# Operand order, a moved transpose and a moved copy at the start of a cross-attention block

## The chip, the cores and the metric

The kernel runs on one core of a Trainium2 chip. The metric is the time of one execution on the device in microseconds (us), as the median of several runs. The core has four engines that compute: TensorE (PE, matrix products and transposes), VectorE (DVE), ScalarE (ACT) and GpSimd (POOL). A fifth, SyncE (SP), issues nearly all data transfers (DMA) here. Each engine works through its own queue of instructions and waits on semaphores for the others. Matrix products are written to PSUM, the accumulators, and copied from there to SBUF, the working memory.

## The reference

All numbers are float32. `x` has 8 sequences of 256 tokens with 512 features; `ctx` has the same shape; the mask is all ones.

```python
x = layer_norm(hidden_states, ln1_w, ln1_b)
q = x @ q_w + q_b
k = encoder_hidden_states @ k_w + k_b
v = encoder_hidden_states @ v_w + v_b            # 16 heads of 32 features each
attn = softmax(where(mask, q k^T / sqrt(32), -max))
out = (attn v) @ cproj_w + cproj_b
hidden = out + residual
y = layer_norm(hidden, ln2_w, ln2_b)
y = gelu(y @ fc_w + fc_b) @ proj_w + proj_b      # 512 -> 2048 -> 512
return hidden + y
```

## The kernel before, in words

The eight sequences are worked in four groups `g` of two, so a group has 512 tokens: four tiles of 128. Weights and transposed tokens are kept as four quarters, "11", "12", "21" and "22", each of 128 partitions x 2 chunks x 256 columns. The first digit of a weight quarter is the half of the outputs and the second the half of the features that are summed over; for tokens the first digit is the half of the features and the second the half of the tokens. Most projections use a Strassen scheme (`strassen`, seven products in place of eight), which needs sums of quarters (`sum_up`, L171). DVE and POOL form these.

The keys of group 0 are the exception. They are needed before any sums can be ready, so `eight` (L455) multiplies the plain quarters. One call makes one quarter of the keys in one PSUM tile of two 256-column halves `i`; it adds over four feature chunks `c`. The profile shows each of these matrix products as two instructions, so a quarter has 16.

The order of all work is written out by hand: each engine's queue is the order in which the Python code calls it. The start of the kernel is this order (L804 and on):

- `warm`: twelve transposes of the identity matrix on PE.
- SP issues the loads: ctx tiles 0 and 1, key weights "11" and "12" (`kw`), ctx tiles 2 and 3, key weights "21" and "22", then x of group 0, the query weights `qw`, the mask, the value weights `vw`, two bias vectors (`cb`, `projb`), ctx of group 1, and the weights `cw` of the output projection. POOL issues eight small loads into `rows`, one 128-wide row for each 128 entries of the bias and scale vectors.
- `turn_first_ctx` (L309) has two pieces. Piece 0 transposes ctx tiles 0 and 1 and makes ctx quarters "11" and "21"; piece 1 transposes tiles 2 and 3 and makes "12" and "22". In each, DVE copies the first quarter (L324) and ACT the second (L326).
- The run `first[0], k[0], first[1], k[1]` puts piece 0 ahead of key quarter "11" and piece 1 between the key quarters "11" and "12".
- In the middle of quarter "12", `turn_cols` (L479) transposes `rows` on PE, and DVE copies the result to `cols`, so that every vector stands as one column per 128 entries. Then ACT adds the key bias, which is one of these columns, to quarter "11", which had waited for it (`waiting`).
- Then come `seen` (layer-norm statistics of x, four tiles, DVE, L194), `roots` (1/sqrt of the variances, POOL, L199 and L200), key quarter "21", `normalise` (DVE, L203), the sums of `qw`, the mask, `tx` (transposes of x on PE, L216, scaled on the way out of PSUM by ACT and DVE), key quarter "22", and the seven query products `q`.

The key quarters "21" and "22" go to DRAM (`store_quarter`, L420); SP issues these stores in its one queue, and `load_x(1)`, the load of x for group 1, stands in that queue behind the second of them. The statistics of x of group 1 are called between the query products, so on DVE they stand between the additions u2 and u3 of the Strassen scheme (L391, L400). After the values, the kernel goes through 32 attention units (scores, softmax, transposed probabilities, product with the values) with the projections of later groups spread between them, and then through the two feed-forward products of each group.

Of the kernel before, what the change touches and what calls it, by code (L numbers as in the profile page):

```python
# [16 lines left out]
P = 128  # L17
# [5 lines left out]
def tile_xattn_block(  # L23
# [45 lines left out]
    nc = tc.nc  # L69
# [9 lines left out]
    NC = D // P  # L79
# [6 lines left out]
    HI, HC, HF, HD2 = INNER // 2, NC // 2, NF // 2, D // 2  # L86
# [27 lines left out]
    n_rows = sum(n for _, n in vecs)  # L114
    rows = const.tile([n_rows, P], F32, name="rows")
    cols = const.tile([P, n_rows], F32, name="cols")
    at, col_of = 0, []
# [6 lines left out]
    def col(base, i):  # L124
        return cols[:, base + i : base + i + 1]
# [4 lines left out]
    QUARTERS = ("11", "12", "21", "22")  # L130
# [87 lines left out]
    def tokens_operand(pool, tag, name):  # L218
        return Operand(pool.tile([P, 7, HC, S], F32, tag=tag, bufs=1, name=name))
# [29 lines left out]
    with ExitStack() as att:  # L249
# [8 lines left out]
        ctxs, xs, att_in, ws, pts = {}, {}, {}, {}, {}  # L258
# [15 lines left out]
        def turned(name):  # L274


            places[0] += 1
            if not pts and (places[0] % 2 or probs):
                return ps_t.tile([P, G], F32, tag="pt", name=name)
            return ps_s.tile([P, G], F32, tag="s", name=name)  # L280
# [28 lines left out]
        def turn_first_ctx():  # L309


            def piece(k):
                if k == 0:
                    ctxT[0] = tokens_operand(both, "cT", "ctxT_0")
                for j in range(2):
                    ps = turned(f"pct_0_{k}_{j}").rearrange("p (c s) -> p c s", c=HC)
                    for t in range(2):
                        for c in range(HC):
                            nc.tensor.transpose(
                                ps[:, c, ts(t, P)], ctxs[0][2 * k + t][:, ts(HC * j + c, P)], ident  # L320
                            )
                    to = ctxT[0][QUARTERS[2 * j + k]]
                    if j == 0:
                        nc.vector.tensor_copy(to, ps)  # L324
                    else:
                        nc.scalar.copy(to, ps)  # L326

            return [lambda k=k: piece(k) for k in range(2)]

        def turn_x(g):  # L330
            def piece(c):
                if c == 0:
                    xnT[g] = tokens_operand(work, "xT", f"xnT_{g}")
                ps = turned(f"pxt_{g}_{c}")
                turn(ps, xs[g], c)
                if g == 0 and c % 2:
                    nc.vector.tensor_scalar(
                        chunk(xnT[g], c), halves(ps), col(c_ln1w, c), col(c_ln1b, c), ALU.mult, ALU.add
                    )
                else:  # L340
                    nc.scalar.activation(
                        chunk(xnT[g], c), halves(ps), AF.Identity,
                        bias=col(c_ln1b, c), scale=col(c_ln1w, c),
                    )

            return [lambda c=c: piece(c) for c in range(NC)]

        turns, later, waiting = [0], [], []
# [68 lines left out]
        def store_quarter(g, tag, o, k, st):  # L417
            d = qkv_dram[g, tag]
            d = d[k * S : (k + 1) * S, ts(o, S)] if tag == "v" else d[o * S : (o + 1) * S, ts(k, S)]
            nc.sync.dma_start(d.rearrange("(i p) s -> p i s", p=P), st)  # L420

        def staged(g, tag, n):
            return work.tile([P, 2, S], F32, tag="st", bufs=3, name=f"st_{tag}_{g}_{n}")

        def project_qk(g, tag):
            w, base = ("k", c_kb) if tag == "kT" else ("q", c_qb)

            def made(n, bank, u):
                o, k = int(n[0]) - 1, int(n[1]) - 1

                direct = g == 0 and o == 0
                st = None if direct else staged(g, tag, n)
                for i in range(2):
                    b = col(base, 2 * o + i)
                    to = qk[g, i, tag][:, ts(k, S)] if direct else st[:, i, :]
                    if u is None:
                        nc.scalar.activation(to, bank[:, i, :], AF.Identity, bias=b, scale=1.0)
                    else:
                        nc.vector.scalar_tensor_tensor(
                            to, bank[:, i, :], b, u[:, i, :], ALU.add, ALU.add  # L440
                        )
                if not direct:
                    store_quarter(g, tag, o, k, st)

            def src():
                return (ctxT if tag == "kT" else xnT)[g]

            if g == 0:
                for i in range(2):
                    qk[g, i, tag] = work.tile([P, G], F32, tag=tag, name=f"{tag}_{g}_{i}")  # L450
            if g == 0 and tag == "kT":
                return [lambda n=n: eight(f"p{tag}_{g}", n, ws[w], src, made) for n in QUARTERS]
            return strassen(f"p{tag}_{g}", lambda: ws[w], src, False, made)

        def eight(name, n, w, x, made):  # L455


            bank = ps_m.tile([P, 2, S], F32, tag=f"m{turns[0]}", name=f"{name}_{n}")
            turns[0] ^= 1
            for i in range(2):  # L460
                if n == "12" and i == 1:

                    turn_cols()
                    waiting.pop()()
                for c in range(NC):
                    nc.tensor.matmul(  # L466
                        bank[:, i, :],
                        w[f"{n[0]}{c // HC + 1}"][:, c % HC, ts(i, P)],
                        x()[f"{c // HC + 1}{n[1]}"][:, c % HC, :],
                        start=i == 0 and c == 0,  # L470
                        stop=c == NC - 1,
                        skip_group_check=True,
                    )
            if n == "11":
                waiting.append(lambda: made(n, bank, None))
            else:
                made(n, bank, None)

        def turn_cols():  # L479
            ps = turned("ps_cols")  # L480
            nc.tensor.transpose(ps[:, :n_rows], rows, ident[:n_rows, :n_rows])
            nc.vector.tensor_copy(cols, ps[:, :n_rows])

        def project_v(g):

            def made(n, bank, u):
                o, k = int(n[0]) - 1, int(n[1]) - 1
                st = staged(g, "v", n)
                if u is None:
                    nc.scalar.copy(st, bank)  # L490
                else:
                    nc.vector.tensor_tensor(st, bank, u, ALU.add)
                store_quarter(g, "v", o, k, st)

            return strassen(f"pv_{g}", lambda: ws["v"], lambda: ctxT[g], True, made)
# [185 lines left out]
        def load_ctx(g):  # L681
            ctxs[g] = load_tiles(work, group_of(ef, g), "ctx", f"ctx_{g}")
# [72 lines left out]
        g = 1  # L755
        begin(g, 0, 3, load_res, 0, *QUARTERS)
        begin(g, 2, 2, bias_res, 0)
        g = 2
# [6 lines left out]
        g = NG - 1  # L765
# [33 lines left out]
        def run(pieces):  # L799
            for p in pieces:  # L800
                p()
# [15 lines left out]
        for to, vec in ((cb, cproj_b), (projb, proj_b)):  # L817
            nc.sync.dma_start(to, vec.partition_broadcast(P))

        first = turn_first_ctx()  # L820
        k, q, v, tx = project_qk(0, "kT"), project_qk(0, "qT"), project_v(0), turn_x(0)
        seen, roots, normalise = layer_norm(xs[0], "a0")
        run([first[0], k[0], first[1], k[1]])
        load_ctx(1)
        ws["c"] = weight("cw", cproj_w)
        run([*seen, roots, k[2], *normalise])
# [71 lines left out]
    with ExitStack() as mlp:  # L898
# [39 lines left out]
        for g in range(NG):  # L938
# [28 lines left out]
            for q in range(HF // 2):  # L967
                bank = {
                    n: ps_f.tile([P, 2, S], F32, tag=f"f{n}", name=f"pf{n}_{g}_{q}") for n in (1, 6, 7, 5)
                }  # L970
# [59 lines left out]
            if g + 1 < NG:  # L1030
# [4 lines left out]
            bank = {  # L1035
                n: ps_f.tile([P, 2, HD2], F32, tag=f"f{n}", name=f"py{n}_{g}") for n in (1, 6, 7, 5)
            }
# [104 lines left out]
```

## Time and profile before

| | us |
|---|---|
| median of 3 runs | 755.97 (755.66 to 756.12) |
| the profiled execution's own time | 755.82 |
| its span, first to last instruction | 754.0 |
| PE busy | 745.0 |
| POOL busy | 380.2 |
| DVE busy | 361.2 |
| ACT busy | 293.4 |
| first key product starts | 6.06 |
| key quarter "12" starts | 10.97 |
| transposes of x start on PE | 18.68 |
| first query product starts | 24.98 |

The profile is of one execution. Times in its views count from the first instruction, and the span is 1.8 us shorter than the execution's own time. A row of a timeline gives the start, the length, the engine, the line of the kernel, and what is written and read; a note in square brackets gives the engine's idle time just before it and who ended it. The chain of waits is followed back from the last instruction: at each step it goes to whatever released that instruction, or to the one ahead of it on the same engine. In the rows of DMA issues the last number is the time from issue to landing.

### The profile page before, as it was taken

How to read it: one execution, taken by the hardware profiler on the slowest of the kernel's cores; microseconds unless marked ns; L12 is line 12 of the kernel's file. 1: busy time of each engine (PE TensorE's matmuls, PEld its weight loads, DVE VectorE, ACT ScalarE, POOL GpSimd, SP SyncE). 2: the span in 40 equal slices, each digit the busy share in tenths (PEclk: the TensorE clock that was granted, in tenths of full speed). 3: DMA queues.
4: the chain of work that ended last, by engine and by line, in shares of the span. 5: the costliest groups of instructions: out<-in, count | busy, mean ns of one | idle time of the engine just before them, and what ended most of it. 6: DMA issues, size and time to landing. Idle time of an engine off the chain costs nothing.

```text
span 754.0 us, 12115 instructions
## 1 busy us (share of the span) xinstructions
PE 745.0 (99%) x4437; PEld 625.1 (83%) x4437; DVE 361.2 (48%) x970; ACT 293.4 (39%) x851; POOL 380.2 (50%) x346
## 2 busy tenths in 40 slices
PE   8999999999999999999999999999999999999997
PEld 7888777888788776778888888888888888888886
DVE  2776755676466566765355542245422255122111
ACT  2277777765776777761341002230013300032100
POOL 3857679677564479896654420126202165012540
PEclk9999999999999999999999999999999999999999
DMA  9714522642234268433930003000040000200001
GB/s 300 227 65 130 166 81 81 185 165 85 85 104 154 85 194 265 129 113 98 295 123 1 1 29 140 1 1 0 1 167 1 1 1 0 82 31 0 1 1 56
DMA packets 60331, 68.70 MB, mean 91 GB/s; under 512 B 5060, under 2 KB 46064, under 8 KB 60144
## 3 DMA queue, kind: packets, MB, share of 16 engines
q1 hardware_dynamic: 60016, 67.91, 27.6%
q8 instruction: 35, 0.57, 0.3%
q14 instruction: 24, 0.20, 0.1%
q0 software_dynamic: 256, 0.02, 0.0%
HBM read 46.95 MB, written 20.97 MB: 90 GB/s over the span
## 4 chain that ended last, share of the span: by engine, by line
PE 94%; ACT 2%; DVE 2%; issue 1%; DMA 1%; POOL 0%; SPq 0%; DVEq 0%; POOLq 0%
PE py L914 26%; PE pf L914 26%; PE ppt L617 7%; PE pqT L367 6%; PE pv L367 5%; PE po L367 5%; PE s L564 5%; PE av L633 5%; PE pkT L367 5%; ACT pr L592 2%; PE pkT L466 1%; PE pyt L216 1%; PE pxt L216 1%; ACT pt L622 1%; PE pct L216 1%
## 5 line engine op out<-in xcount | busy, mean ns | idle before, releaser
L914 PE MATMUL pf<-y,fcw 128*128 128x256 f32 x896 | 194.0, 379 | 0.0
L914 PEld LDWEIGHTS pf<-y,fcw 128*128 128x128 f32 x896 | 170.2, 190 | 23.1
L606 POOL TENSOR_TENSOR pr<-pr,rsum 128x512 f32<-128x512 f32 x128 | 130.3, 1050 | 75.5 <-DVE rsum L604 44.3
L592 ACT ACTIVATE pr<-pr,nmax 128x256 f32<-128x256 f32 x256 | 128.1, 503 | 61.3 <-DVE nmax L582 61.2
L1018 POOL TENSOR_TENSOR hs<-h,h 128x512 f32<-128x512 f32 x16 | 20.3, 1268 | 192.4 <-PE pf L914 146.7
L582 DVE CUSTOM_DVE_ANT_0 pr<-s,mb 128x256 f32<-128x256 f32 x256 | 94.1, 413 | 42.0 <-PE s L564 32.8
L914 PE MATMUL py<-pw,h 128*128 128x256 f32 x384 | 85.1, 380 | 0.0
L914 PE MATMUL py<-pw_t,h 128*128 128x256 f32 x384 | 83.5, 379 | 0.0
L914 PEld LDWEIGHTS py<-pw,h 128*128 128x128 f32 x384 | 72.7, 190 | 10.0
L914 PEld LDWEIGHTS py<-pw_t,h 128*128 128x128 f32 x384 | 72.7, 190 | 9.8
L993 ACT COPY u<-pf 128x512 f32<-128x512 f32 x16 | 9.4, 586 | 166.3 <-PE pf L914 164.7
L617 PEld LDWEIGHTS ppt<-ident,pr 128*128 128x128 f32 x512 | 57.3, 141 | 14.8 <-issue 9.9
L617 PE MATMUL ppt<-ident,pr 128*128 128x128 f32 x512 | 68.7, 276 | 0.2
L622 ACT COPY pt<-ppt 128x512 f32<-128x512 f32 x96 | 51.7, 572 | 4.9 <-PE ppt L617 4.9
L977 ACT ACTIVATE h<-h,cols 128x256 f32<-128x256 f32 x96 | 43.4, 501 | 25.8 <-DVE h L1014 13.3
L367 PE MATMUL pv<-vw,ctxT 128*128 128x256 f32 x224 | 52.4, 380 | 0.0
L977 ACT ACTIVATE h<-pf,cols 128x256 f32<-128x256 f32 x32 | 13.4, 471 | 99.6 <-PE pf L914 99.6
L367 PE MATMUL pqT<-xnT,qw 128*128 128x256 f32 x224 | 51.0, 379 | 0.0
L592 ACT ACTIVATION_READ_ACCUMULATOR pr<-pr,nmax 128x1 f32 x256 | 48.5, 189 | 0.0
L367 PEld LDWEIGHTS pqT<-xnT,qw 128*128 128x128 f32 x224 | 41.4, 190 | 5.0
L367 PEld LDWEIGHTS pv<-vw,ctxT 128*128 128x128 f32 x224 | 41.0, 190 | 5.4 <-issue 0.3
L633 PE MATMUL av<-pt,v 128*32 128x256 f32 x512 | 38.9, 386 | 1.3 <-ACT pt L622 0.4
(132 smaller groups left out, 966.9 us busy)
## 6 DMA issues: line engine op xcount, KB each, us to landing
ctx<-in_ctx_dram SPq DMA_DIRECT2D x16, 256.0 KB, 4.6
x<-in_x_dram SPq DMA_DIRECT2D x16, 256.0 KB, 4.1
v_dram<-st_v SPq DMA_DIRECT2D x16, 256.0 KB, 2.2
v<-v_dram SPq DMA_DIRECT2D x16, 256.0 KB, 3.7
resx<-in_x_dram SPq DMA_DIRECT2D x16, 256.0 KB, 5.2
hid_dram<-resx SPq DMA_DIRECT2D x16, 256.0 KB, 2.3
hm<-hid_dram SPq DMA_DIRECT2D x16, 256.0 KB, 5.9
fcw<-in_L_xattn_fc_w_dram SPq DMA_DIRECT2D x16, 256.0 KB, 6.0
```

What stands on the lines that cost most here:

```text
L216: nc.tensor.transpose(ps[:, ts(t, P)], xt[:, ts(c, P)], ident)
L367: nc.tensor.matmul(bank[n][:, i, :], l[:, c, ts(i, P)], r[:, c, :], start=first and i == 0 and c == 0, stop=last and c == HC - 1, skip_gro ...
L564: nc.tensor.matmul(banks[j][:, i, :], qT[j * HD : (j + 1) * HD, b * S + i * P : b * S + (i + 1) * P], kT[j * HD : (j + 1) * HD, b * SK : ( ...
L582: nc.vector.tensor_tensor_reduce(pr[:, j, i, :], banks[j][:, i, :], mbias[g][1][:, b, :], scale=-SCALE, scalar=FLT_MAX, op0=ALU.add, op1=A ...
L592: nc.scalar.activation(pr[:, j, i, :], pr[:, j, i, :], AF.Exp, bias=nmax[:, j, i : i + 1], scale=-1.0, accum_out=sums[:, j, i : i + 1],)
L606: nc.gpsimd.tensor_tensor(pr[:, j], pr[:, j], rsum[:, j, :, None].to_broadcast([P, NQ, SK]), ALU.mult,)
L617: nc.tensor.transpose(ps[:, kc, ts(i, P)], probs[n][:, j, i, ts(kc, P)], ident)
L622: nc.scalar.copy(pt, ps)
L633: nc.tensor.matmul(av[j * HD : (j + 1) * HD, :], vs[g, hg][:, b * NK + kc, ts(j, HD)], pts[n, j][:, kc, :], start=(kc == 0), stop=(kc == N ...
L914: nc.tensor.matmul(ps, lhsT, rhs, start=first, stop=last, skip_group_check=True)
L977: nc.scalar.activation(h[n][q][:, i, :], src[:, i, :], AF.Gelu_apprx_tanh, bias=col(c_fcb, half * HF + 2 * q + i), scale=1.0,)
L1018: nc.gpsimd.tensor_tensor(h["s3"][q], h["11"][q], h["21"][q], ALU.subtract)
```

## The change

Three things are changed, all in the first four key quarters and the call that runs them.

- `eight` goes through the products in another order: first all that read the first half of the features (both column halves `i`), then all that read the second half. The number of products is the same. A table of `hooks` may name places between products at which something else is run.
- The second piece of the ctx transposes is no longer called between the key quarters "11" and "12". It is run inside quarter "11", ahead of its seventh product (of eight).
- The vectors are turned ahead of the fifth product of quarter "12", as before, but their copy out of PSUM is made by ACT in place of DVE.

```diff
-                return [lambda n=n: eight(f"p{tag}_{g}", n, ws[w], src, made) for n in QUARTERS]
+                return [lambda n=n: eight(f"p{tag}_{g}", n, ws[w], src, made, FIRST_KEYS.get(n, {})) for n in QUARTERS]
...
-        def eight(name, n, w, x, made):
+        def eight(name, n, w, x, made, hooks):
...
-            for i in range(2):
-                if n == "12" and i == 1:
-
-                    turn_cols()
-                    waiting.pop()()
-                for c in range(NC):
-                    nc.tensor.matmul(
-                        bank[:, i, :],
-                        w[f"{n[0]}{c // HC + 1}"][:, c % HC, ts(i, P)],
-                        x()[f"{c // HC + 1}{n[1]}"][:, c % HC, :],
-                        start=i == 0 and c == 0,
-                        stop=c == NC - 1,
-                        skip_group_check=True,
-                    )
+
+            for at, (j, i, c) in enumerate((j, i, c) for j in range(2) for i in range(2) for c in range(HC)):
+                if at in hooks:
+                    hooks[at]()
+                nc.tensor.matmul(
+                    bank[:, i, :],
+                    w[f"{n[0]}{j + 1}"][:, c, ts(i, P)],
+                    x()[f"{j + 1}{n[1]}"][:, c, :],
+                    start=at == 0,
+                    stop=j == 1 and c == HC - 1,
+                    skip_group_check=True,
+                )
...
+        def turn_second_half():
+            first_ctx[1]()
+
+        def turn_vectors():
+
+            turn_cols()
+            waiting.pop()()
+
+        FIRST_KEYS = {"11": {6: turn_second_half}, "12": {4: turn_vectors}}
+
         def turn_cols():
             ps = turned("ps_cols")
             nc.tensor.transpose(ps[:, :n_rows], rows, ident[:n_rows, :n_rows])
-            nc.vector.tensor_copy(cols, ps[:, :n_rows])
+            nc.scalar.copy(cols, ps[:, :n_rows])
...
-        first = turn_first_ctx()
+        first_ctx = turn_first_ctx()
...
-        run([first[0], k[0], first[1], k[1]])
+        run([first_ctx[0], k[0], k[1]])
```

## The prediction

> **What bounds the kernel now.** I read the page first (busy shares), then the chain that ended last in order of time, because the change touches only the first 23 us and a share over the whole span hides them.
>
> ```profile
> PE 745.0 (99%) x4437; PEld 625.1 (83%) x4437; DVE 361.2 (48%) x970; ACT 293.4 (39%) x851; POOL 380.2 (50%) x346
> ```
>
> TensorE (PE) is busy 745 of 754 us, so only what moves PE's own stream counts. The chain over the first 26 us:
>
> ```profile
> 1.65 4.27 DMA kw<-in_L_xattn_k_w_dram
> 5.92 0.14 issue
> 6.06 3.69 PE pkT L466 x16
> 9.75 0.45 PE pct L319 x4
> ...
> 10.22 0.70 DVE ctxT L324
> 10.93 0.04 issue
> 10.97 1.99 PE pkT L466 x8
> ...
> 13.19 0.20 DVE cols L482
> 13.39 0.61 DVE st_a L194
> ...
> 17.00 1.05 POOL rstd_a L200
> ...
> 18.54 1.47 DVE x L203 x3
> 20.00 0.04 issue
> 20.05 1.64 PE pxt L216 x13
> 21.69 3.46 PE pkT L466 x16
> ```
>
> The chain leaves PE twice. At 10.2 it goes to VectorE (DVE), which copies the turned ctx half for quarter "12". At 13.2 it goes to DVE and GpSimd (POOL) for x's layer norm and returns at 20.05. A matmul here is two instructions; 16 in 3.46 us means one per 0.216 us. After 25 us the chain is PE almost without a break to 53.6.
>
> The size of the second hole: quarters "12" and "21" end at 13.18 + 24 x 0.216 = 18.36 (13.08, plus 0.10 of restart). The 16 turns of x at 0.109 would end at 20.10; the next quarter starts at 21.53. Lost: 1.42 us. Why is the norm late? From the timeline of DVE, then the DMA issues in the window 4.65 to 4.75:
>
> ```profile
> 10.22 0.69 DVE L324 COPY ctxT<-pct 128x512 f32<-128x512 f32 x1 [4.76 <-PE pct L319]
> 13.19 0.20 DVE L482 COPY cols<-ps_cols 128x44 f32<-128x44 f32 x1 [2.27 <-PE ps_cols L481]
> 13.31 0.68 DVE L194 BATCH_NORM_STATS2 st_a<-x 128x6 f32<-128x512 f32 x1
> ```
> ```profile
> x<-in_x_dram SPq DMA_DIRECT2D x1, 256.0 KB, 5.9
> ```
>
> x's first tile was issued at 4.60 and landed 5.9 us later, at 10.5. DVE was free at 10.9, but the copy of the turned vectors stood ahead of the statistics in its queue and waited 2.27 us for PE.
>
> [...]statistics whose data lay there waited behind a copy. [...]the keys' store at 21.20 landed only 7.2 us later behind the loads ahead of it, the one at 26.05 in 2.7.
>
> **The change part by part.**
>
> *Order of the first quarter.* The old order used kw "12" from its fifth instruction, the new from its ninth. kw "11" landed at 5.92 and started PE; kw "12", issued at 2.12, landed 4.5 us later at 6.6, and the fifth instruction started about 6.9 without a wait. So the order itself is worth 0. ScalarE's (ACT) copy of ctx "21" ended at 5.8, also hidden. In quarter "12" the order only puts off the need for ctx "22" (ACT's copy ended at 11.24) to instruction nine.
>
> *Second half of ctx turned inside the quarter.* The 8 turns (0.87 us) move from behind 16 instructions to behind 12, from 9.59 to 6.06 + 0.07 + 12 x 0.216 = 8.72. The tiles they need were issued at 2.63 and 3.10 and landed 4.9 and 5.0 later, 7.5 and 8.1: no wait, 0.6 to spare. DVE's copy started 0.64 after the first turn and PE went on 0.75 after that start: 8.72 + 0.64 + 0.75 = 10.11. Meanwhile PE ends the turns at 9.59 and the last four key instructions at 10.46. So quarter "12" starts at 10.46 without a wait, against 10.97, and its restart (second instruction 0.32 after the first, not 0.216) goes too: **0.61 us** gained. Cover gone (copy over 0.35 late): the old wait returns in part, at most 0.61. No DMA is moved.
>
> *Turned vectors, copied by ACT.* They still stand after eight instructions of quarter "12", now about 12.3. The last bias row, issued at 5.36, landed 5.8 later at 11.2: no wait. The gap of about 0.4 around this 44-row turn stays. On ACT the copy ([...]below nothing it can't be, above it 0.3 by the 0.586 of a twelve times larger copy) runs about 12.6 to 12.8, then the two bias additions for quarter "11" (0.84) to 13.7. Behind them only quarter "21" waits, which needs the bank at 14.3: 0.6 to spare, so 0. ACT has nothing else queued. DVE loses 0.20.
>
> *What that frees.* DVE ends ctx "12" at 10.05 and begins the statistics when x lands, 10.6. They need 0.80 a tile; the fourth tile landed at 12.4 and is wanted at 13.0. From the first statistics to the roots took 13.31 to 18.05 = 4.74, so normalising runs 15.4 to 17.3 (1.92). POOL was idle for 10.8 us ahead of it. PE ends quarter "21" at 18.36 - 0.61 = 17.75 and finds all four tiles: **1.42 us** gained, 0.45 to spare. Without ACT's copy, DVE's would stand at 12.6 and about 1.4 of this be lost again.
>
> *What is late next.* PE's x turns 17.75 to 19.50, last key quarter to 22.95, queries from there (24.98 before): 2.03. DVE's sums end 17.3 + 5.35 (20.00 to 25.35 before) = 22.65, wanted by the second product at 24.7. POOL's sums follow DVE's and move 2.5 to 2.7. These are free. The exception is load_x(1): SyncE (SP) issues it behind the store of the last key quarter, so it moves from 26.52 to 24.5, but its tiles then queue behind cw and the stores. On DVE its statistics stand ahead of u3, which the sixth query product needs:
>
> ```profile
> 29.38 0.69 DVE L194 BATCH_NORM_STATS2 st_a<-x 128x6 f32<-128x512 f32 x1
> 31.05 0.69 DVE L194 BATCH_NORM_STATS2 st_a<-x 128x6 f32<-128x512 f32 x1 [0.76 <-DMA x<-in_x_dram]
> 32.09 0.69 DVE L400 TENSOR_TENSOR pqT_u<-pqT,pqT_u 128x512 f32<-128x512 f32 x1
> ```
> ```profile
> x<-in_x_dram SPq DMA_DIRECT2D x1, 256.0 KB, 4.0
> ```
>
> The second tile was issued at 27.03 and landed 4.0 later, 31.03. In the new time the sixth product starts at 22.95 + 5 x 1.73 = 31.6, so u3 must start by 30.9 and the second statistics (0.93 ahead) by 29.9. Earliest: issue at 25.0 plus the store's 2.7 as shortest landing, 27.7; no loss. Latest: unmoved, 31.05; loss 1.1 plus 0.1 restart, 1.2. Taken: the first tile no earlier than about 29.3, since the last quarter of cw, issued at 20.34, landed only 7.1 later[...]; and the second statistics 0.80 after it, 30.1: **0.2 lost**.
>
> Sum: 0.61 + 1.42 - 0.2 = 1.83. The profiled execution took 755.82 (span 754.0, 1.8 around it), so 753.99. The median of the runs shown is 0.15 higher: 754.14, said as **754.1**.
>
> **Rivals.**
>
> *Whole shift.* x(1) lands in time: 2.03 gained, 753.9. For: DMA was near idle at 26 to 27, so the tiles can start a microsecond earlier.[...] With 0.5 lost instead it is 754.4; I count both as the forecast.
>
> *x(1) sets the queries.* It lands where it did: 2.03 - 1.2 = 0.83, 755.1.
>
> *The norm does not move.* DVE or POOL is held by something unshown, and only the 0.61 stays: 755.4. Against: no wait on anything but PE stands ahead of the statistics.
>
> *Slower: x(1) later than before.* The same place and price: each us past 29.9 for the second statistics stops PE for one. It decides at 29.9 + 2.03 = 31.9, 0.9 later than in the profile, where new and old are even; from 33.4 it costs over 0.2%. For: the loads enter busier DMA queues.[...]
>
> *More.* The attention stage has waits of ACT in PE's weight loads (9.6 us before the attention products); another phase there could add or take 0.3 to 0.5: 753.5.
>
> **How the numbers follow.** Forecast with its spread 753.8 to 754.4: 0.57. More than that gained: 0.10. x(1) sets the queries, or a part of the gain is lost later: 0.17. Norm doesn't move: 0.10. Slower: 0.06. About 0.2% (1.5 us) is what a measurement of this kernel can tell from no change; 754.46 is that bound. Faster is the first two and a third of the third: 0.72; same 0.22; slower 0.06. The range 753.5 to 755.3 leaves out the slower case and the far ends.
>
> **What would show it.** Right: turns of ctx at 8.7, key quarter "12" at 10.5 with no wait on DVE; statistics at 10.6 waiting on DMA, not PE; x's turns at about 17.8 with no idle time; queries at about 23.0; everything from 35 us on early by one amount. Wrong: PE idle in the queries behind u3 with x(1) named; a wait on ctx inside the first quarter; bias additions holding quarter "21"; or the early amount shrinking through the attention units.

## The result, and the profile after

The changed kernel takes 754.29 us (median of 12 runs, 753.90 to 755.44), the kernel before 756.06 us in the same comparison (12 runs). The ratio is 0.9977, with a 95% interval of 0.9968 to 0.9986: 1.8 us or 0.23% faster. The forecast was 754.1, in a range of 753.5 to 755.3. The profiled execution of the changed kernel took 754.31 us, with a span of 752.5.

The page's row of busy time, changed kernel: TensorE does the same work in a shorter span.

```profile
PE 744.8 (99%) x4437; PEld 626.2 (83%) x4437; DVE 360.5 (48%) x969; ACT 293.1 (39%) x852; POOL 380.0 (50%) x346
```

The chain of waits in order of time, changed kernel (start, length, what):

```profile
1.64 4.42 DMA kw<-in_L_xattn_k_w_dram
6.06 0.14 issue
6.19 3.18 PE pkT L464 x12
9.37 0.87 PE pct L319 x8
10.25 2.59 PE pkT L464 x12
12.84 0.19 PE ps_cols L489
13.03 5.38 PE pkT L464 x24
18.40 1.75 PE pxt L216 x16
20.15 3.46 PE pkT L464 x16
23.61 12.16 PE pqT L367 x56
```

Both of the chain's ways out of PE are gone: it stays on PE from the landing of the key weights on. The second half of ctx is turned behind 12 key instructions and key quarter "12" follows without a gap. The 16 turns of x follow quarter "21" at once.

The timeline of DVE, changed kernel, shows why the norm is no longer late:

```profile
9.85 0.69 DVE L324 COPY ctxT<-pct 128x512 f32<-128x512 f32 x1 [4.09 <-PE pct L319]
11.04 0.69 DVE L194 BATCH_NORM_STATS2 st_a<-x 128x6 f32<-128x512 f32 x1 [0.49 <-DMA x<-in_x_dram]
15.82 1.92 DVE L203 TENSOR_SCALAR x<-x,mv_a,rstd_a 128x512 f32<-128x512 f32 x4 [1.49 <-POOL rstd_a L200]
```

The statistics wait for the landing of x and for nothing else, where they waited for PE's turn of the vectors before. They start at 11.04 in place of 13.31.

What is due to the change and what to the execution? PE's timeline, first of the kernel before, then of the changed one:

```profile
3.98 1.20 PE L319 MATMUL pct<-ident,ctx 128*128 128x128 f32 x8
6.06 3.69 PE L466 MATMUL pkT<-ctxT,kw 128*128 128x256 f32 x16 [0.88 <-DMA kw<-in_L_xattn_k_w_dram]
24.98 12.25 PE L367 MATMUL pqT<-xnT,qw 128*128 128x256 f32 x56
```
```profile
3.97 1.91 PE L319 MATMUL pct<-ident,ctx 128*128 128x128 f32 x8
6.19 3.18 PE L464 MATMUL pkT<-ctxT,kw 128*128 128x256 f32 x12 [0.31 <-DMA kw<-in_L_xattn_k_w_dram]
23.44 12.33 PE L367 MATMUL pqT<-xnT,qw 128*128 128x256 f32 x56
```

The queries start 1.54 us sooner. But the same eight ctx turns took 1.91 us here and 1.20 before: PE runs at half pace at first (its warming transposes start 0.213 us apart in both profiles, later ones 0.109). The trace's record of the granted clock has full speed from 6.9 us on in this execution, against 4.3. So the first two key instructions took 0.86 us, start to start, in place of 0.51. The key weights also landed at 6.06 in place of 5.92. These two, 0.35 and 0.13, belong to the execution. Without them the queries would start at 22.96, where the prediction had 22.95. From there the lead holds: the first scores stand at 37.43 against 38.89 (1.46), and the spans differ by 1.5.

### The profile page after: what moved, and what is told of

Same layout as the page of the kernel before. It is cut to its first block, busy times and chain, and to the rows that moved or that the text cites. A ratio compares the mean times of both kernels' runs of the same rounds, so it can differ in the third digit from the quotient of the medians.

```text
span 752.5 us, 12116 instructions
## 1 busy us (share of the span) xinstructions
PE 744.8 (99%) x4437; PEld 626.2 (83%) x4437; DVE 360.5 (48%) x969; ACT 293.1 (39%) x852; POOL 380.0 (50%) x346
## 4 chain that ended last, share of the span: by engine, by line
PE 94%; ACT 2%; DMA 2%; DVE 1%; issue 0%; SPq 0%; DVEq 0%
PE py L922 26%; PE pf L922 26%; PE ppt L625 7%; PE pqT L367 6%; PE pv L367 6%; PE s L572 5%; PE po L367 5%; PE pkT L367 5%; PE av L641 5%; PE pkT L464 2%; ACT pr L600 1%; PE pyt L216 1%; PE pxt L216 1%; PE pct L216 1%; DMA kw<-in_L_xattn_k_w_dram 1%; ACT pt L630 1%
```

## The experiments

**One part alone: the ScalarE copy.** The kernel before with one line changed.

```diff
-            nc.vector.tensor_copy(cols, ps[:, :n_rows])
+            nc.scalar.copy(cols, ps[:, :n_rows])
```

> The kernel before, with only the copy of the turned vectors moved from VectorE to ScalarE. My theory, that x's layer norm is late because its statistics stand behind that copy: the statistics start at about 11.0 (when VectorE has copied the second ctx half) in place of 13.3, the turns of x follow quarter "21" without idle time at about 18.4, and the time falls by 1.4 us, less up to 0.3 if the load of x for group 1 then holds the queries. Rival, that moving the ctx turns does most of the work: under 0.5 us faster.

Measured: 754.72 us (21 runs) against 755.94 for the kernel before on the same chip; ratio 0.9981 (0.9975 to 0.9988), 1.2 us faster. Its chain of waits still leaves PE for the ctx copy, and no longer for the norm:

```profile
10.03 0.70 DVE ctxT L324
10.73 0.04 issue
10.78 1.99 PE pkT L466 x8
12.77 0.18 PE ps_cols L481
12.96 5.38 PE pkT L466 x24
18.33 1.75 PE pxt L216 x16
```

So the larger part of the gain, two thirds, comes from one 0.2 us copy that left DVE's queue. The rival falls. The size of the hole is as worked out, too: from the start of quarter "12" to that of quarter "22" it is 10.56 us in the profile before (10.97 to 21.53) and 9.14 here (10.78 to 19.92), 1.42 less.

**The other part alone: ctx turned inside the quarter.** The changed kernel with that line given back to DVE.

> The changed kernel, with the copy of the turned vectors given back to VectorE. My theory: key quarter "12" starts without a wait, some 0.6 us sooner, and the statistics stay behind the vectors' copy and come 0.6 us sooner as well, so the time is 0.6 us below before and x's turns still wait about 1.4 us. Rival, that the ctx turns are the larger part: over 1.2 us faster.

Measured: 755.21 us (21 runs) against 755.94; ratio 0.9991 (0.9984 to 0.9997), 0.7 us faster. The norm is late again, for the reason named, in the timelines of DVE and of PE:

```profile
13.06 0.20 DVE L490 COPY cols<-ps_cols 128x44 f32<-128x44 f32 x1 [2.52 <-PE ps_cols L489]
13.18 0.68 DVE L194 BATCH_NORM_STATS2 st_a<-x 128x6 f32<-128x512 f32 x1
```
```profile
18.55 3.01 PE L216 MATMUL pxt<-ident,x 128*128 128x128 f32 x16 [0.15 <-DVE x L203]
```

PE takes 3.01 us for turns that take 1.91 when nothing holds them, and idles before them too. From the middle of quarter "12" to the start of quarter "22" 1.41 is lost against the changed kernel (12.95 to 21.39, against 12.96 to 19.99). The two parts alone gain 1.2 and 0.7, together 1.9; the whole gained 1.5, 1.8 and 2.0 in its three comparisons. That is additive within what these runs tell.

**Is it ScalarE, or the place in the queue?** DVE keeps the copy, but three of x's four statistics are called ahead of it.

```diff
-            nc.scalar.copy(cols, ps[:, :n_rows])
+            nc.vector.tensor_copy(cols, ps[:, :n_rows])
...
-        run([first_ctx[0], k[0], k[1]])
+        run([first_ctx[0], k[0], *seen[:3], k[1]])
...
-        run([*seen, roots, k[2], *normalise])
+        run([seen[3], roots, k[2], *normalise])
```

> The changed kernel, with the copy of the turned vectors on VectorE again, but three of x's four statistics called ahead of it. My theory, that what counts is the place of the statistics in VectorE's queue and not the engine of the copy: the statistics start when x lands (10.4 to 11.0), the copy stands behind three of them at about 13.0, x's turns do not wait, and the time is that of the changed kernel within 0.3. Rival, that ScalarE must make the copy: as with the copy given back, 0.7 below before.

Measured: 754.22 us (13 runs), with the changed kernel at 754.29 (13 runs) and the one before at 755.83 on the same chip. The same time with this copy on DVE: what counted was the order of DVE's queue.

The timeline of DVE in this kernel:

```profile
10.85 0.69 DVE L194 BATCH_NORM_STATS2 st_a<-x 128x6 f32<-128x512 f32 x1 [0.28 <-DMA x<-in_x_dram]
13.27 0.17 DVE L490 COPY cols<-ps_cols 128x44 f32<-128x44 f32 x1
```

**The order of the first products.** The changed kernel with the products of a key quarter in the old order.

```diff
-            for at, (j, i, c) in enumerate((j, i, c) for j in range(2) for i in range(2) for c in range(HC)):
+            for at, (j, i, c) in enumerate((j, i, c) for i in range(2) for j in range(2) for c in range(HC)):
```

> The changed kernel, with the products of each first key quarter in the old order (one column half over all four chunks, then the other); the ctx turns stay ahead of the seventh product and the ScalarE copy stays. My theory, the order is worth nothing as long as the key weights "12" land before the fifth instruction: as the changed kernel within 0.2 us, 1.6 to 2.0 below before; where they land late (they landed at 7.03 in the profile of the changed kernel) a few tenths are lost. Rival, the order does a part of the gain: 0.5 us or more slower than the changed kernel.

Measured: 754.28 us (11 runs) against 755.94 before; ratio 0.9978 (0.9969 to 0.9987), 1.7 us faster. The changed kernel itself was not run on this chip; in its three comparisons it was 1.5 to 2.0 faster. So the order named first in the change does nothing that the times can tell.

The profile of this run is less plain. The rows are PE's weight loads (PEld, one for each instruction), and the DMA issue of the key weights "12" (window 2.15 to 2.25):

```profile
5.79 0.73 PEld L464 LDWEIGHTS pkT<-ctxT,kw 128*128 128x128 f32 x4 [0.58 <-DVE ctxT L324]
6.98 1.59 PEld L464 LDWEIGHTS pkT<-ctxT,kw 128*128 128x128 f32 x8 [0.46 <-issue]
```
```profile
kw<-in_L_xattn_k_w_dram SPq DMA_DIRECT2D x1, 256.0 KB, 4.8
```

Those weights were issued at 2.11 and landed at 6.9. The fifth instruction, the first that reads them in the old order, started at 7.01, where 6.76 was due. With the restart (0.10 in the profile before) that is a loss of 0.3 us, which the expectation had named for weights that land late. The trace names no releaser for this wait, but the landing fits it. The two other profiles with the old order lost at most 0.02 there, and none with the new order waited for these weights. So the new order covers a wait that comes in some executions; what it is worth in the median is not resolved.

**Is x of group 1 the next bound?** The forecast took 0.2 us off for it. First its load was issued sooner.

```diff
-        run([*tx, k[3]])
-        load_x(1)
+        run(tx)
+        load_x(1)
+        run([k[3]])
```

> The changed kernel, with the load of x for group 1 issued ahead of the last key quarter and its store, as soon as x's turns free the tiles (at about 21.8 in place of 25.0). My theory, that these tiles now land just at the limit and cost the median run 0.2: their statistics on VectorE start by 28 and the time falls by 0.1 to 0.3 below the changed kernel, 1.9 to 2.1 below before. Rival, that they have slack in most runs: no difference from the changed kernel, 1.7 to 1.8 below before.

Measured: 754.17 us (8 runs), 1.8 below before, which is inside what the changed kernel gained elsewhere (it was not run on this chip). So the theory's 0.1 to 0.3 cannot be seen. But the early landing, which was to test it, did not come either. The issues of x in the window 21.9 to 22.0:

```profile
x<-in_x_dram SPq DMA_DIRECT2D x1, 256.0 KB, 6.8
```

Issued at 21.8, three us sooner, the first tile took 6.8 us and the statistics began at 28.70, where the changed kernel has 29.27 to 30.10 in its three profiles. The loads of cw stood ahead of it: the last of them, issued at 20.27, took 7.1 us as well. So the load was moved ahead of cw:

```diff
-        ws["c"] = weight("cw", cproj_w)
         run([*seen, roots, k[2], *normalise])
...
-        run([*tx, k[3]])
-        load_x(1)
+        run(tx)
+        load_x(1)
+        ws["c"] = weight("cw", cproj_w)
+        run([k[3]])
```

> The changed kernel, with the load of x for group 1 issued ahead of the four loads of cw, which are not wanted before the attention units. In the earlier try the load was issued sooner but landed at the same 29.3, behind cw. Here the tiles should land by 26, the statistics should wait for nothing but TensorE, and if late tiles cost the changed kernel anything, the time falls 0.1 to 0.3 below it. If not: the same within 0.1.

> The kernel with x of group 1 loaded ahead of cw once more, since five runs were few: 0.1 to 0.3 below the changed kernel on the same chip if late tiles cost it that; within 0.1 if not.

(The earlier try did not land at 29.3, as the first of these texts says, but at 28.6.) Measured: 753.95 us (5 runs) with the changed kernel at 754.19 (6 runs) beside it; then 754.09 (10 runs) with the changed kernel at 754.29 (13 runs). Both are 0.2 lower, which is what was expected, but the single runs overlap, and so do the intervals against the kernel before (0.9955 to 0.9980 and 0.9966 to 0.9984) and those of the changed kernel (0.9959 to 0.9982 and 0.9969 to 0.9985). The times alone do not show the gain. Two profiles show what can be lost. First the timelines of PE and of DVE of the changed kernel in its third profile, then those of the kernel with x ahead of cw in its second:

```profile
23.32 8.80 PE L367 MATMUL pqT<-xnT,qw 128*128 128x256 f32 x40
32.48 3.69 PE L367 MATMUL pqT<-xnT,qw 128*128 128x256 f32 x16 [0.36 <-issue]
```
```profile
30.10 0.69 DVE L194 BATCH_NORM_STATS2 st_a<-x 128x6 f32<-128x512 f32 x1 [2.36 <-DMA x<-in_x_dram]
31.72 0.66 DVE L400 TENSOR_TENSOR pqT_u<-pqT,pqT_u 128x512 f32<-128x512 f32 x1
```
```profile
23.44 12.25 PE L367 MATMUL pqT<-xnT,qw 128*128 128x256 f32 x56
```
```profile
27.77 0.68 DVE L194 BATCH_NORM_STATS2 st_a<-x 128x6 f32<-128x512 f32 x1
```

In the first kernel, the first tile landed at 30.1, u3 began at 31.72, and PE stopped ahead of the sixth product, as the prediction had it. The 56 instructions took 12.85 us. Without waits they take 12.25, as in the second kernel. In the changed kernel's other two profiles they took 12.33 and 12.26, so the loss is 0.08, 0.01 and 0.60: 0.2 in the mean of three, and between nothing and 0.6 from one execution to the next. Three other kernels here issue these loads in the same order and reach the queries about as early. In their profiles, the one with the old order lost 0.13, and the ones with the copy alone and with the statistics called ahead lost nothing.

With x ahead of cw, the first tile was issued at 19.85 and landed 6.0 us later, at 25.9. It was issued sooner than in the first try because the four issues of cw, which keep SP for 2.85 us in the first profile of the changed kernel, now stood behind it. So the loads ahead of it and its time of issue were not separated.

**The statistics of x of group 1 called later on DVE.**

```diff
-        for i in range(4):
-            run([q[i + 1], seen[i]])
+        run([*q[1:4], seen[0], q[4], *seen[1:]])
```

> The changed kernel, with the statistics of x of group 1 called later on VectorE: the first one behind the addition u3, the other three behind the fourth query product's results. If late tiles of x cost the changed kernel its last 0.1 to 0.3 us, by holding u3: faster by that much than the changed kernel, with no idle time of TensorE in the 56 query instructions (12.25 long). If not: the same within 0.1.

A miss: 755.35 us (21 runs), 1.2 slower than the changed kernel. The queries took 12.25 without a wait, as expected. The stop came behind them: three statistics now stood ahead of the sixth product's results, whose bank the first value product takes next.

The timeline of PE and DVE behind the queries:

```profile
35.49 0.86 DVE L439 SCALAR_TENSOR_TENSOR st_qT<-pqT,cols,pqT_u 128x256 f32<-128x256 f32 x2
36.40 0.91 PE L367 MATMUL pv<-vw,ctxT 128*128 128x256 f32 x3 [0.70 <-DVE st_qT L439]
```

The queries start at 23.46, as in the first profile of the changed kernel (23.44), and the first scores at 38.33 in place of 37.43. So 0.9 is lost here. Another 0.4 goes at 231 us in this profile, in one attention unit; why is not known.

**The slower rival made to happen.** Three stores of 256 KB ahead of x of group 1 in SP's queue. Their data are quarters of the value weights, written to a scratch tensor that nothing reads.

```diff
+    dump_dram = {n: tc.dram_tile([P, 2, S], F32, name=f"dump_dram_{n}") for n in ("11", "12", "21")}
...
         run([*tx, k[3]])
+        for n in QUARTERS[:3]:
+            nc.sync.dma_start(dump_dram[n], ws["v"][n])
         load_x(1)
```

> The changed kernel, with three more stores of 256 KB each (a quarter of the value weights to a scratch tensor) ahead of the load of x for group 1 in SyncE's queue. This is the slower rival of the prediction made to happen: the tiles land about 2 us later, u3 waits for them, and the sixth query product stops TensorE. Theory of the price (each us past the limit of 29.9 costs one): the time rises by 1.5 to 2.2 us over the changed kernel and is as before or slightly slower. Rival, that the delay is made up in the attention units: under 0.5 us over the changed kernel.

Measured: 756.41 us (13 runs) against 754.19 of the changed kernel and 756.23 before: 2.2 over the changed kernel, at the upper end of the expectation, and the gain is gone. In its profile u3 starts at 32.98 and the sixth product at 33.73, where 23.64 + 8.63 = 32.27 was due (timeline; its line numbers are one higher):

```profile
31.35 0.69 DVE L195 BATCH_NORM_STATS2 st_a<-x 128x6 f32<-128x512 f32 x1 [3.29 <-DMA x<-in_x_dram]
32.98 0.66 DVE L401 TENSOR_TENSOR pqT_u<-pqT,pqT_u 128x512 f32<-128x512 f32 x1
33.73 3.48 PE L368 MATMUL pqT<-xnT,qw 128*128 128x256 f32 x15 [1.29 <-issue]
```

That stop costs 1.46 us. The second statistics, at 32.18, stood about 1.5 past their limit, which moves with the queries (32.27 less 0.75 for u3 and 0.80 for the statistics), so each us past it cost one, as the prediction had it. POOL's sums of the value weights also had to wait 3.2 us for these stores, but only about 0.1 is lost on PE from the sixth product to the end. Against the first profile of the changed kernel, whose span is 2.1 shorter, the rest is 0.2 ahead of the queries, where the clock rose later (7.4), and 0.3 behind the last matrix product: the execution ends 4.0 us after DVE's last addition, in place of 3.7. What makes this end longer is open.

**The clock at the start.** One warming transpose in place of twelve, and the changed kernel beside it.

```diff
-        for t in range(12):
+        for t in range(1):
             nc.tensor.transpose(warm[:, ts(t % NT, P)], ident, ident)
```

> The changed kernel with one warming transpose in place of twelve. Theory, that TensorE's clock comes to full speed some 3 to 6 us after it starts to be busy, at a moment that differs between executions, and that this alone made the first key instructions slow in the changed kernel's profile: full speed comes about 2 us later than in the other profiles (4.3 to 7.4 there), and each us costs about a half, so 0.6 to 1.2 us over the changed kernel. Rival, that the warming is idle work: no difference.

> The changed kernel itself, for comparison on the same chip as the next three. 1.6 to 1.8 us below before. In the profile at hand its first three key instructions took 0.86 us in place of 0.50 because the TensorE clock came to full speed at 6.9 us and not at 4.3; in another execution that moment should lie elsewhere, and the queries then start between 22.8 and 23.4.

> The changed kernel itself, beside the three others on the same chip: 1.6 to 2.0 below before.

Measured: 755.70 us (12 runs, 754.35 to 757.17) with one warming transpose, 1.4 over the changed kernel (754.29), a little more than expected. In the profile the queries start at 24.48, 1.0 to 1.4 later than in the three of the changed kernel. The changed kernel itself took 754.19 (6 runs) and 754.29 (13 runs). The first twelve key instructions, with one warming transpose and then in the second profile of the changed kernel:

```profile
5.90 4.51 PE L464 MATMUL pkT<-ctxT,kw 128*128 128x256 f32 x12
```
```profile
6.19 2.83 PE L464 MATMUL pkT<-ctxT,kw 128*128 128x256 f32 x12 [0.80 <-DMA kw<-in_L_xattn_k_w_dram]
```

By the trace's record the clock rose at 9.3 with one warming transpose; up to there the key instructions start 0.43 us apart, and 0.216 behind it. In the three profiles of the changed kernel it rose at 6.9, 4.6 and 7.0, with the queries at 23.44, 23.09 and 23.32.

## Why the prediction was right

Order of the first quarter, 0: right for the profile that it was read from, and for the times. But it rested on 0.3 us between the landing of the key weights "12" (6.6) and their use (6.9), and first landings differ by more than that between executions: the old order waited 0.25 in another one. It should have been said as "0 to 0.3".

Second half of ctx inside the quarter, 0.61: right. Alone it measured 0.7, and quarter "12" started without a wait in all profiles with it. The slack of 0.35 that the step named was enough.

Turned vectors, copied by ACT, 0: right. The copy took 196 ns. That it would take about 0.2 us was the author's estimate: the profile before has no such copy on ACT; its two of 512 columns took 586 ns each (L326). The key bias followed at 13.29, and quarter "21" didn't wait for its bank.

What that frees, 1.42: right in mechanism, and in size: the copy alone gained 1.2 in the times and closed 1.42 in its profile. The statistics started as x landed. The 0.45 us to spare for x's turns was enough in every profile, though x landed up to 0.6 later than in the profile before (its statistics began at 11.18 in one). The sentence that about 1.4 would be lost again without ACT's copy is only half of it: with the statistics called ahead of the copy, nothing is lost on DVE either. In that run the copy stood behind three statistics and started at 13.27, though PE had turned the vectors by 13.06.

What is late next, 0.2: right in place and mechanism, and the least certain term. The mean over three profiles is 0.2, and with x ahead of cw the medians were 0.2 lower in two comparisons, which their spread does not tell from nothing. That the first tile lands behind cw, however early it is issued, was the author's estimate. Measured: behind cw, a tile issued three us sooner (21.8, against 24.98 in the first profile of the changed kernel) landed about one us sooner (the statistics that waited for it began at 28.70, against 29.70). Neither end was met in the changed kernel's profiles: no tile landed near 27.7, and no loss came near 1.2.

Of the rivals, "x(1) sets the queries" is true of one profile of three, at half its price. "The norm does not move" is what the second experiment shows, with ACT's copy taken away: 755.2 against the 755.4 worked out. "More" did not come: the lead of 1.46 at the first scores is the lead of the spans.

The three comparisons gained 1.5, 1.8 and 2.0, so they carry the terms, but not the agreement to 0.2 us of 754.1 with 754.29; that close, it is partly luck.

What the prediction did not have is the clock. It took the first 6 us of one profile as fixed, and that profile had the earliest rise of all. The later rise cost 0.35 us in the profile after. Nothing in the change moves this rise, so it should hit the medians of both kernels alike, though no run here shows that. A comparison of single profiles it did hit: 1.54 where 2.03 was due.

## What to carry to other kernels

In the kernel before, a copy that waited 2.27 us for PE held the statistics behind it in DVE's queue, though x had landed at 10.5 and DVE was free at 10.9: look at the head of the queue when a long chain of small work starts late, and either move the waiting instruction to an engine with nothing behind it or call the ready work ahead of it. When such a repair moves a stretch of a kernel forward, list the loads that don't move with it; here a load issued three us sooner landed only one us sooner behind the loads ahead of it, so ask what stands ahead of it, and not only when it is issued. A term put at nothing because of a few tenths to spare in one profile may be something in the next. And before two profiles are compared in tenths of a us, compare the same instructions at their start, for the clock and the first landings differ between executions.

## What was not expected of the hardware

PE's clock rose to full speed at a different moment in each profile: between 4.3 and 7.4 us with twelve warming transposes from 1.35 on, and at 9.3 with one. The same eight transposes of ctx took 1.20 to 1.91 us by it. Why the moment moves is not shown. Loads also landed at times that differ between executions. The statistics that waited for the first tile of x began between 10.42 and 11.18. The first key weights held PE until 6.19 in the first profile of the changed kernel; in its third, PE began on them at 5.81 without a wait. And the statistics that waited for x of group 1 began at 29.27 to 30.10 in the three profiles of the changed kernel, with the loads ahead of it the same.
